# Sending half of the first batch's inner products by GpSimd's queue, and moving one chunk of the keys between two groups' scores

## The chip, the cores and the metric

The kernel runs on one core of one Trainium2 chip. The core has five engines that run beside one another: TensorE (PE in the profile) multiplies matrices, VectorE (DVE) and ScalarE (ACT) work element by element and on rows, GpSimd (POOL) does the same more slowly, and SyncE (SP) only issues transfers (DMAs). ACT and POOL issue transfers too. Each engine works through its own list of instructions in order: if one has to wait, all behind it on that engine wait with it. The metric is the time of one execution on the chip, in microseconds (us).

## The reference

For each of 8 batches there are 112 rows of queries (320 channels) and 375 rows of context (512 channels). The last 4 context rows are image prompts, the other 371 are text. There are 20 heads of 16 channels. In short form, with the mask called `m`:

```python
q, k, v   = x @ W_q, text @ W_k, text @ W_v          # by heads
probs     = softmax(q k^T / 4)                        # 112 x 371 for each head
text_out  = probs @ v
qsem      = l2norm(probs @ text)                      # 112 x 512 for each head
sem       = qsem @ l2norm(prompts)^T                  # 112 x 4 for each head
fused     = q (prompts @ W_k_ip)^T / 4 + 0.5 * sem
ip_out    = (softmax(fused) * m) @ (prompts @ W_v_ip)
out       = (text_out + ip_out) @ W_out + b_out + x
```

## The kernel before

The norm of `probs @ text` is not computed from the 512 channels. With the inner products of the context rows, `G = text text^T`, the squared norm is `p G p^T`, so for each head the kernel multiplies the probabilities by a matrix `u` whose columns are half of G (one triangle, doubled off the diagonal), then the inner products with the prompts, a column of ones and the head's 16 value channels. One product of 112 x 371 by 371 x 392 thus gives the norm, the prompts' part, the sum of the exponentials and the values. This is line 761 (`ps_qd<-u,xgT`).

TensorE works on 32 rows at a time there, four heads beside one another: a *group* is 4 heads, each batch has 5 groups, each group 12 blocks of 32 text rows. For that `u` has to lie in each of the four groups of 32 partitions (the *row groups*), and so has the transposed probability matrix `xgT`.

The names that matter for the first batch, in the order in which they come about:

- `first_gram` multiplies the turned context by itself (L491). `doubled` (L508 on ACT, L513 on POOL) writes the result to `ug`, 128 partitions of 792 columns.
- `gram_to_groups` (L543) copies `ug` to `u`: for each quarter `q` of its 128 partitions, four transfers of 99 KB, one for each row group. Four quarters make 16 transfers.
- `values` (L598) computes the values, ACT copies them to `vext` (L605), a transfer on ACT's queue writes them to `vd` in DRAM (L611), and `values_to_groups` (L632, four transfers on SP's queue) reads them back as `vr`. `placed` (L679, POOL) copies `vr` into its columns of `u`. The first of these copies needs all of `u` and all of `vr`.
- `project_queries` (L391) gives `qm` in three chunks of channels. The third, `ps_q_2`, reads columns of `wq_sb` that a copy on POOL fills (line 1090 before, 1091 after).
- `keys` (L559 and L576) gives `kT` in three chunks, `ps_k_0`, `ps_k_1` and `ps_k_2`. Groups 0 and 1 read the first chunk of `qm` and `kT`, groups 2 and 3 the second, group 4 the third.
- `scores` (L713) and `probabilities` (maximum L726 on DVE, exponential L730 on ACT, then a transfer `xg<-p`, L737 on SP) run per head. A score goes to one of the 8 banks of TensorE's output memory and can only start when that bank's former reader is done. `transposed` (L749, DVE) makes `xgT` of the group's four transfers, for group 0 in two halves of 6 blocks.
- `gram(1)` (L529) computes the inner products of batch 1, which `doubled` writes to the same `ug`, as soon as all 16 transfers have read it.
- After the prologue `alone(0)` runs group 0's 48 products with the scores of group 2 between them; then come a value chunk and a key chunk of batch 1, and `prompt_projections` (L304), which needs the weights `wip`. Those are two transfers of 640 KB (L125) on SP's queue, behind the transfers of group 1's probabilities.

The order of the prologue on each engine is the order in which the code is written; a generator such as `run(("k", 0), None)` emits one piece of its stage at a time.

Of the kernel before, what the change touches and what calls it, by code (L numbers as in the profile page):

```python
# [20 lines left out]
def kernel(  # L21
# [14 lines left out]
    nc = tc.nc  # L36
# [27 lines left out]
    QN = P // RG  # L64
# [105 lines left out]
    def load_turned(eng, bs):  # L170

        t0, n = blocks_of(bs)
        rows = x.rearrange("b s c -> (b s) c")[t0 : t0 + n * RG, :]
        for q in range(QN):
            eng.dma_start(
                x_in[q * RG : (q + 1) * RG, :n, :XW],
                rows[:, q * XW : (q + 1) * XW].rearrange("(j i) c -> i j c", i=RG),
            )
# [261 lines left out]
    def transposed_context(b):  # L440
        begin(b)
        s = st[b]
        ct, ctxT = s["ct"], s["ctxT"]
        if b > 0:

            for c in range(NT):
                some = slice(c * QN, (c + 1) * QN)
                nc.vector.transpose(  # L448
                    ctxT[:, :, c * P : (c + 1) * P].rearrange("p e (j i) -> p j e i", i=RG),
                    ct[:, some, :].rearrange("p j (k e) -> p j e k", e=NE),  # L450
                )
                if c == NT - 1:
                    prompts_behind(b)
                yield
            return
        for c in range(NT):
            rows = min(P, TT - c * P)
            ps = bank(f"ps_c_{b}_{c}")
            for e in range(NE):
                nc.tensor.transpose(  # L460
                    ps[:, e * P : e * P + rows],
                    chunk(ct[:, c, :], e)[:rows],
                    ident[:rows, :rows],
                )
            o = ctxT[:, :, c * P : c * P + rows]
            i = ps.rearrange("p (e t) -> p e t", t=P)[:, :, :rows]
            if c % 2:
                nc.vector.tensor_copy(o, i)
            else:
                nc.scalar.copy(o, i)  # L470
            yield
# [64 lines left out]
            doubled(ps, c, c, DEAL[c] if left_out(b, c) else ())  # L536
            yield

    def gram_to_groups(b, blocks):

        for q in blocks:
            for a in range(GROUP):
                nc.sync.dma_start(  # L543
                    st[b]["u"][a * RG : (a + 1) * RG, q * GW : (q + 1) * GW],
                    ug[q * RG : (q + 1) * RG, :],
                )
# [44 lines left out]
    def values(b):  # L591
        s = st[b]
        s["vext"] = work.tile([P, NT, C], F32, tag="vext", name=f"vext_{b}", bufs=1)
        ctxT, vext = s["ctxT"], s["vext"]
        for c in range(NT):
            ps = bank(f"ps_v_{b}_{c}")
            for e in range(NE):
                nc.tensor.matmul(  # L598
                    ps[:, :C],
                    ctxT[:, e, c * P : (c + 1) * P],  # L600
                    wv_sb[:, e, :],
                    start=(e == 0),
                    stop=(e == NE - 1),
                )
            nc.scalar.copy(vext[:, c, :], ps[:, :C])  # L605
            yield
# [68 lines left out]
    def placed(b, g, chunks=range(NT)):  # L675

        s = st[b]
        for c in chunks:
            nc.gpsimd.tensor_copy(  # L679
                region(b, c)[:, :, UV - c * P :], s["vr"][:, c * QN : (c + 1) * QN, g, :]  # L680
            )
# [19 lines left out]
    def scores(b, g, a, early=False, ps=None):  # L701
        s = st[b]
        _, qm, j = queries[b]
        i, r = g // 2, g % 2
        if early and (g + a // 2) % 2:

            ps = ps_qd.tile([P, 512], F32, tag="qd", name=f"ps_s_{b}_{g}_{a}")
        elif ps is None:
            ps = ps_sc.tile([P, 512], F32, tag="sc", name=f"ps_s_{b}_{g}_{a}")
        w = T if b > 0 else TT  # L710
        if i == FULL:
            r = a // 2
        nc.tensor.matmul(  # L713
            ps[:S, :w],
            qm[a * RG : (a + 1) * RG, i, r, j * S : (j + 1) * S],
            s["kT"][a * RG : (a + 1) * RG, i, :w],
            start=True,
            stop=True,
        )
        s["sc", g, a] = ps  # L720

    def probabilities(b, g, a):
        s = st[b]
        ps = s.pop(("sc", g, a))
        nmx = small.tile([S, 1], F32, tag="nmx", name=f"nmx_{b}_{g}_{a}", bufs=8)
        nc.vector.tensor_reduce(nmx, ps[:S, :TT], AX.X, ALU.max, negate=True)  # L726
        if ("p", g) not in s:
            s["p", g] = work.tile([S, GROUP, TT], F32, tag="p", name=f"p_{b}_{g}", bufs=4)
        p = s["p", g][:, a, :]
        nc.scalar.activation(p, ps[:S, :TT], AF.Exp, bias=nmx)  # L730
        if b > 0:
            nc.scalar.copy(s["ipl"][:, groups[g][a], :], ps[:S, TT:T])  # L732

        xg = x_ring[(b * NG + g) % NX]
        rows = xg[a * RG : a * RG + S // QN, :, :TT]
        eng = nc.scalar if (b, g, a) == (B - 1, NG - 1, GROUP - 1) else nc.sync
        eng.dma_start(rows, p)  # L737
# [315 lines left out]
    def drain(*gens):  # L1053
        for gen in gens:
            for _ in gen:
                pass
# [5 lines left out]
    def run(key, make, pieces=1):  # L1062

        if key not in gens:
            gens[key] = make()
        for _ in range(pieces):
            next(gens[key], None)
# [15 lines left out]
    turned_inputs(pairs[0])  # L1083
    drain(products)
    drain(transposed_context(1))
    gram_to_groups(0, range(QN - 1))
    run(("v", 0), lambda: values(0))
    run(("v", 0), None, 2)
    values_to_dram(0, nc.scalar)
# [5 lines left out]
    for a in range(GROUP):  # L1095
        scores(0, 0, a, early=True)
        probabilities(0, 0, a)
    gram_to_groups(0, (QN - 1,))
    run(("q", 0), None)
    for a in range(GROUP):  # L1100
        scores(0, 1, a, early=True)
        probabilities(0, 1, a)
# [1 line left out]
    load_embed(nc.sync, wvip_sb, w_v_ip)  # L1104
    transposed(0, 0)
    placed(0, 0)
    run(("k", 0), None, 2)
    load_turned(nc.gpsimd, pairs[1])
    more_constants()
    turn[:] = ["mm", "mm", "sc"]  # L1110
# [121 lines left out]
    def moved(b, g):  # L1232

        nb = b + 1
        if b % 2 == 0:
            if g in (1, 2):
                gram_to_groups(nb, (g - 1,))
            if g == 3:
                todo = [lambda: gram_to_groups(nb, (3,)), lambda: values_to_groups(nb)]
                for move in reversed(todo) if nb == B - 1 else todo:  # L1240
                    move()
        else:
            if g in (0, 1):
                gram_to_groups(nb, (g,))
            if g == 2:
                values_to_groups(nb, 0, 2)
# [114 lines left out]
    for n in range(0, len(steps) - NG, 2):  # L1361
# [4 lines left out]
        b, g = steps[n]  # L1366
# [16 lines left out]
    b = B - 1  # L1383
# [125 lines left out]
```

## Time and profile before

| what | us |
|---|---|
| three runs | 410.67, 411.17, 412.36 |
| median of the runs | 411.17 |
| span of the profiled execution | 409.5 |
| TensorE busy in that span | 402.0 |
| VectorE busy | 333.5 |
| ScalarE busy | 191.4 |
| GpSimd busy | 127.6 |

The span runs from the first to the last instruction of one profiled execution. The time of that one execution is not given apart from its span; the median of the runs lies 1.6 us above the span, and this is used for what lies around it. In the profile's rows of instructions in order of time the columns are start, duration, engine, line, operation, names, shapes and how many were merged; in brackets stands how long the engine was idle before and what ended that. `SPq` and `ACTq` are instructions that issue transfers on those queues; POOL's transfers are listed under POOL.

### The profile page before, as it was taken

How to read it: one execution, taken by the hardware profiler on the slowest of the kernel's cores; microseconds unless marked ns; L12 is line 12 of the kernel's file. 1: busy time of each engine (PE TensorE's matmuls, PEld its weight loads, DVE VectorE, ACT ScalarE, POOL GpSimd, SP SyncE). 2: the span in 40 equal slices, each digit the busy share in tenths (PEclk: the TensorE clock that was granted, in tenths of full speed). 3: DMA queues.
4: the chain of work that ended last, by engine and by line, in shares of the span. 5: the costliest groups of instructions: out<-in, count | busy, mean ns of one | idle time of the engine just before them, and what ended most of it. 6: DMA issues, size and time to landing. Idle time of an engine off the chain costs nothing.

```text
span 409.5 us, 14124 instructions
## 1 busy us (share of the span) xinstructions
PE 402.0 (98%) x5603; PEld 316.1 (77%) x5603; DVE 333.5 (81%) x705; ACT 191.4 (47%) x676; POOL 127.6 (31%) x294
## 2 busy tenths in 40 slices
PE   8998999999999999999999999999999999999996
PEld 8866687978777877878686877778777878787894
DVE  4354589877999898896899898887799988878985
ACT  3253234344533743434643574333734485346763
POOL 7203311322281153011154136002037135104681
PEclk9999999999999999999999999999999999999999
DMA  8876957799666866677646776666756444666310
GB/s 234 166 188 170 231 145 193 170 196 208 150 162 163 215 141 177 156 165 163 180 115 167 177 174 161 166 160 161 180 152 173 114 123 121 191 159 179 106 49 28
DMA packets 59332, 65.83 MB, mean 161 GB/s; under 512 B 20165, under 2 KB 52793, under 8 KB 59268
## 3 DMA queue, kind: packets, MB, share of 16 engines
q1 hardware_dynamic: 55326, 59.11, 58.4%
q0 software_dynamic: 1456, 3.14, 3.5%
q10 hardware_dynamic: 2486, 2.69, 2.1%
q8 instruction: 44, 0.72, 0.8%
q14 instruction: 20, 0.16, 0.1%
HBM read 20.22 MB, written 5.22 MB: 62 GB/s over the span
## 4 chain that ended last, share of the span: by engine, by line
PE 92%; DMA 3%; SPq 2%; POOL 1%; ACT 1%; issue 0%; DVE 0%; POOLq 0%
PE ps_qd L761 44%; PE ps_v L598 12%; PE ps_k L559 10%; PE ps_g L529 7%; PE ps_s L713 6%; PE ps_q L391 3%; PE ps_o L917 3%; DMA wip<-in_L_xattn_W_v_ip_dram 3%; PE ps_k L576 2%; PE ps_g L491 1%; SPq L737 1%; PE ps_w L477 1%; PE ps_c L460 1%; SPq L543 1%; PE ps_q L373 1%; PE ps_o L1013 0%
## 5 line engine op out<-in xcount | busy, mean ns | idle before, releaser
L761 PE MATMUL ps_qd<-u,xgT 32*112 32x136 f32 (+11 forms) x3840 | 216.4, 352 | 1.5 <-POOL u L679 1.1
L761 PEld LDWEIGHTS ps_qd<-u,xgT 32*112 32x112 f32 x3840 | 178.1, 172 | 36.4 <-issue 7.1
L749 DVE STREAM_TRANSPOSE xgT<-xg 128x768 f32<-128x768 f32 (+1 forms) x63 | 123.1, 1972 | 5.4 <-DMA xg<-p 5.1
L730 ACT ACTIVATE p<-ps_s,nmx 112x371 f32<-112x371 f32 x160 | 85.7, 585 | 56.9 <-DVE nmx L726 55.7
L726 DVE TENSOR_REDUCE nmx<-ps_s 112x1 f32<-112x371 f32 x160 | 77.2, 534 | 30.8 <-PE ps_s L713 28.9
L679 POOL COPY u<-vr 128x64 f32<-128x64 f32 x120 | 26.8, 237 | 190.9 <-PE ps_qd L761 113.8
L814 DVE CUSTOM_DVE_ANT_0 p<-ps_qd,p 112x371 f32<-112x371 f32 x152 | 73.6, 541 | 12.1 <-ACT pvs L788 7.4
L713 PE MATMUL ps_s<-kT,qm 32*112 32x375 f32 (+1 forms) x320 | 62.6, 485 | 0.0
L598 PE MATMUL ps_v<-wv_sb,ctxT 128*128 128x320 f32 x192 | 55.6, 437 | 0.0
L788 ACT COPY pvs<-ps_qd 112x21 f32<-112x21 f32 x152 | 21.8, 200 | 56.7 <-DVE ss L814 50.4
L598 PEld LDWEIGHTS ps_v<-wv_sb,ctxT 128*128 128x128 f32 x192 | 35.7, 190 | 14.3
L559 PE MATMUL ps_k<-ctxT,wk_sb 128*128 128x371 f32 x128 | 43.5, 483 | 0.0
L559 PEld LDWEIGHTS ps_k<-ctxT,wk_sb 128*128 128x128 f32 x128 | 23.1, 190 | 13.4 <-issue 1.3
L713 PEld LDWEIGHTS ps_s<-kT,qm 32*112 32x112 f32 x320 | 28.1, 171 | 5.7 <-ACT ug L508 0.4
L529 PE MATMUL ps_g<-ctxT 128*32 128x119 f32 (+11 forms) x672 | 32.4, 338 | 0.0
L529 PEld LDWEIGHTS ps_g<-ctxT 128*32 128x32 f32 x672 | 27.6, 109 | 5.9 <-issue 2.5
L448 DVE STREAM_TRANSPOSE ctxT<-ct 128x512 f32<-128x512 f32 x21 | 22.4, 1082 | 6.0 <-DMA u<-ug 6.0
L605 ACT COPY vext<-ps_v 128x320 f32<-128x320 f32 x24 | 10.2, 426 | 33.1 <-PE ps_v L598 24.5
L732 ACT COPY ipl<-ps_s 112x4 f32<-112x4 f32 x140 | 24.3, 173 | 0.0
L513 POOL TENSOR_TENSOR ug<-ug,half 128x128 f32<-128x128 f32 (+1 forms) x24 | 10.6, 448 | 29.7 <-ACT ug L512 27.6
L566 ACT COPY kT<-ps_k 128x371 f32<-128x371 f32 x16 | 7.5, 469 | 23.2 <-PE ps_k L559 22.8
L896 POOL TENSOR_TENSOR wv<-vip,w 112x1280 f32<-112x1280 f32 (+1 forms) x8 | 17.5, 2184 | 0.3 <-DVE w L890 0.3
(152 smaller groups left out, 326.0 us busy)
## 6 DMA issues: line engine op xcount, KB each, us to landing
xg<-p SPq DMA_DIRECT2D x159, 162.3 KB
u<-ug SPq DMA_DIRECT2D x128, 99.0 KB
ct<-in_ctx_dram SPq DMA_DIRECT2D x28, 176.0 KB
vip<-vipd SPq DMA_DIRECT2D x7, 560.0 KB
vr<-vd SPq DMA_DIRECT2D x20, 120.0 KB
out_dram<-ob SPq DMA_DIRECT2D x7, 140.0 KB
vd<-vext ACTq DMA_DIRECT2D x12, 80.0 KB
vr<-vd SPq DMA_DIRECT2D x12, 80.0 KB
```

The lines of the kernel that those rows point to most:

```text
L448: nc.vector.transpose(ctxT[:, :, c * P : (c + 1) * P].rearrange("p e (j i) -> p j e i", i=RG), ct[:, some, :].rearrange("p j (k e) -> p j ...
L529: nc.tensor.matmul(ps[p * RG : (p + 1) * RG, s0 : T - t0], ctxT[:, e, t0 + q * RG : t0 + (q + 1) * RG], ctxT[:, e, t0 + s0 : T], start=(e ...
L559: nc.tensor.matmul(ps[:, :TT], wk_sb[:, e, i * P : (i + 1) * P], s["ctxT"][:, e, :TT], start=(e == 0), stop=(e == NE - 1),)
L598: nc.tensor.matmul(ps[:, :C], ctxT[:, e, c * P : (c + 1) * P], wv_sb[:, e, :], start=(e == 0), stop=(e == NE - 1),)
L679: nc.gpsimd.tensor_copy(region(b, c)[:, :, UV - c * P :], s["vr"][:, c * QN : (c + 1) * QN, g, :])
L713: nc.tensor.matmul(ps[:S, :w], qm[a * RG : (a + 1) * RG, i, r, j * S : (j + 1) * S], s["kT"][a * RG : (a + 1) * RG, i, :w], start=True, st ...
L726: nc.vector.tensor_reduce(nmx, ps[:S, :TT], AX.X, ALU.max, negate=True)
L730: nc.scalar.activation(p, ps[:S, :TT], AF.Exp, bias=nmx)
L732: nc.scalar.copy(s["ipl"][:, groups[g][a], :], ps[:S, TT:T])
L749: nc.vector.transpose(xT[:, j : j + n].rearrange("p j (k q) -> p q j k", q=QN), xg[:, :, j * RG : (j + n) * RG].rearrange("p q (j k) -> p ...
L761: nc.tensor.matmul(banks[a][:S, j * RG : UW], xT[a * RG : (a + 1) * RG, j, :S], region(b, c)[a * RG : (a + 1) * RG, p, q * RG :], start=(j ...
L814: nc.vector.tensor_tensor_reduce(out=p, in0=ps[:S, :TT], in1=p, scale=1.0, scalar=0.0, op0=ALU.mult, op1=ALU.add, accum_out=s["ss"][:, h : ...
```

## The change

Two things move in the first batch's prologue, and nothing is added or taken out of the computation. `gram_to_groups` gets a parameter for the engine that issues. The 16 transfers of `ug` were issued by SP, twelve directly after `ug` was made and four behind the probabilities of group 0. Now SP issues eight directly, and POOL the other eight (quarters 2 and 3), at its place in the program. The keys' second chunk, which stood with the third behind the scores of group 1, now stands ahead of them.

```diff
-    def gram_to_groups(b, blocks):
+    def gram_to_groups(b, blocks, eng=nc.sync):
 
         for q in blocks:
             for a in range(GROUP):
-                nc.sync.dma_start(
+                eng.dma_start(
                     st[b]["u"][a * RG : (a + 1) * RG, q * GW : (q + 1) * GW],
                     ug[q * RG : (q + 1) * RG, :],
                 )
...
     drain(transposed_context(1))
-    gram_to_groups(0, range(QN - 1))
+    gram_to_groups(0, (0, 1))
+    gram_to_groups(0, (2, 3), nc.gpsimd)
     run(("v", 0), lambda: values(0))
...
     for a in range(GROUP):
         scores(0, 0, a, early=True)
         probabilities(0, 0, a)
-    gram_to_groups(0, (QN - 1,))
     run(("q", 0), None)
+    run(("k", 0), None)
     for a in range(GROUP):
         scores(0, 1, a, early=True)
         probabilities(0, 1, a)
...
     placed(0, 0)
-    run(("k", 0), None, 2)
+    run(("k", 0), None)
     load_turned(nc.gpsimd, pairs[1])
```

In the lists below a number behind a name is only its place in the program, and `x4` is four equal instructions. First TensorE before, from the last score of group 0 (`ps_s_0_3`) over the third query chunk and group 1's scores (`ps_s_1_*`) to the keys' chunks:

```order
L713 MATMUL ps_s_0_3_350<-kT_168,qm_305 112x371
L391 MATMUL ps_q_2_360<-xT_222,wq_sb 128x112 x3
L713 MATMUL ps_s_1_0_367<-kT_168,qm_305 112x371
L713 MATMUL ps_s_1_1_374<-kT_168,qm_305 112x371
L713 MATMUL ps_s_1_2_380<-kT_168,qm_305 112x371
L713 MATMUL ps_s_1_3_386<-kT_168,qm_305 112x371
L559 MATMUL ps_k_1_400<-ctxT_166,wk_sb 128x371 x4
L576 MATMUL ps_k_2_406<-ctxT_166,wk_sb 64x186
```

The same place on TensorE now:

```order
L713 MATMUL ps_s_0_3_354<-kT_168,qm_309 112x371
L391 MATMUL ps_q_2_360<-xT_222,wq_sb 128x112 x3
L559 MATMUL ps_k_1_367<-ctxT_166,wk_sb 128x371 x4
L713 MATMUL ps_s_1_0_373<-kT_168,qm_309 112x371
L713 MATMUL ps_s_1_1_380<-kT_168,qm_309 112x371
L713 MATMUL ps_s_1_2_386<-kT_168,qm_309 112x371
L713 MATMUL ps_s_1_3_392<-kT_168,qm_309 112x371
L576 MATMUL ps_k_2_406<-ctxT_166,wk_sb 64x186
```

The four matmuls of `ps_k_1` have moved ahead of the four scores; `ps_q_2` still stands ahead of both.

GpSimd before, from its part of the first inner products (L513) over the prompts' copy behind batch 1's context (L436) to the next loads:

```order
L513 TENSOR_TENSOR ug<-ug,half 128x115
L436 COPY ctxT_259<-ipnT 128x4x4
L1090 COPY wq_sb<-wq_sb 128x3x64
L679 COPY u_170<-vr_171 128x4x16 x3
L175 DMA x_in<-in_x_dram 32x7x80 x4
```

The same place on GpSimd now:

```order
L513 TENSOR_TENSOR ug<-ug,half 128x115
L436 COPY ctxT_259<-ipnT 128x4x4
L543 DMA u_170<-ug 32x792 x8
L1091 COPY wq_sb<-wq_sb 128x3x64
L679 COPY u_170<-vr_171 128x4x16 x3
L175 DMA x_in<-in_x_dram 32x7x80 x4
```

The eight issues stand behind the copy of L436, which waits for DVE, and ahead of the copy into `wq_sb` on which `ps_q_2` waits.

SP's queue before, from the loads of batch 1's context (L143) to the prompts' weights:

```order
L143 DMA ct_112<-in_ctx_dram 19x128 x4
L543 DMA u_170<-ug 32x792 x12
L632 DMA vr_171<-vd_169 32x12x80 x4
L737 DMA xg_140<-p_0_335 28x4x371 x4
L543 DMA u_170<-ug 32x792 x4
L737 DMA xg_142<-p_1_371 28x4x371 x4
L125 DMA wip<-in_L_xattn_W_k_ip_dram 128x1280
L125 DMA wip<-in_L_xattn_W_v_ip_dram 128x1280
```

The same place on SP's queue now:

```order
L143 DMA ct_112<-in_ctx_dram 19x128 x4
L543 DMA u_170<-ug 32x792 x8
L632 DMA vr_171<-vd_169 32x12x80 x4
L737 DMA xg_140<-p_0_339 28x4x371 x4
L737 DMA xg_142<-p_1_377 28x4x371 x4
L125 DMA wip<-in_L_xattn_W_k_ip_dram 128x1280
L125 DMA wip<-in_L_xattn_W_v_ip_dram 128x1280
```

Eight transfers of `ug` have left SP's queue, four from ahead of `vr` and four from between the probabilities of the two groups.

## The prediction

> **What bounds the kernel now.** I read the page first, for the shares of the engines.
>
> ```profile
> span 409.5 us, 14124 instructions
> PE 402.0 (98%) x5603; PEld 316.1 (77%) x5603; DVE 333.5 (81%) x705; ACT 191.4 (47%) x676; POOL 127.6 (31%) x294
> ```
>
> TensorE counts as busy nearly throughout, so there are two ways to gain time: remove the few waits that are left, or remove time that counts as busy but is stretched. The waits of TensorE, in the view of who waited for whom, are five; these two lie where the change is:
>
> ```profile
> PE ps_qd L761 <- POOL u L679: 1.1, 1, 1.1
> PE ps_kv L304 <- DMA wip<-in_L_xattn_W_v_ip_dram: 0.4, 1, 0.4
> ```
>
> Stretched time shows only in the rows in order of time. TensorE from group 0's scores to the first product of group 0, with one weight load (PEld) and the prompts' projection at the end:
>
> ```profile
> 24.05 0.89 PE L713 MATMUL ps_s<-kT,qm 32*112 32x371 f32 x8
> 24.87 0.92 PE L391 MATMUL ps_q<-xT,wq_sb 128*128 128x112 f32 x6
> 25.72 1.77 PE L713 MATMUL ps_s<-kT,qm 32*112 32x371 f32 x8
> 27.42 2.76 PE L559 MATMUL ps_k<-ctxT,wk_sb 128*128 128x371 f32 x8
> 30.11 1.47 PE L576 MATMUL ps_k<-ctxT,wk_sb 128*64 128x186 f32 x16
> 31.52 4.65 PE L529 MATMUL ps_g<-ctxT 128*32 128x375 f32 x96
> 37.25 0.93 PE L761 MATMUL ps_qd<-u,xgT 32*112 32x392 f32 x8 [1.08 <-POOL u L679]
> ...
> 38.62 0.17 PEld L713 LDWEIGHTS ps_s<-kT,qm 32*112 32x112 f32 x1 [0.44 <-ACT ug L508]
> ...
> 49.04 1.28 PE L304 MATMUL ps_kv<-wip,ipT 128*32 128x160 f32 x28 [0.42 <-DMA wip<-in_L_xattn_W_v_ip_dram]
> ```
>
> Taken from start to start, the same eight score instructions need 0.82 us in group 0 (24.05 to 24.87) and 1.70 us in group 1 (25.72 to 27.42): group 1's wait there for banks that group 0's exponentials still read. So 0.88 us is stretch. Then TensorE idles 1.08 us ahead of group 0's products, because GpSimd places the values late, and that because the last four blocks of `u` land late; ScalarE waits for the same transfers before it may overwrite `ug`:
>
> ```profile
> 36.95 0.59 POOL L679 COPY u<-vr 128x64 f32<-128x64 f32 x3 [15.72 <-DMA u<-ug]
> ...
> 37.06 0.40 ACT L508 ACTIVATE ug<-ps_g 128x279 f32<-128x279 f32 x1 [4.15 <-DMA u<-ug]
> ```
>
> Being late there, ScalarE also holds a bank that a score of group 2 needs (the 0.44 us at 38.62). What that stage loses in all is seen beside a later one of the same make, two groups with their eight scores in 50.25 to 61.10:
>
> ```profile
> core 0: us, PE busy (x), PEclk, DMA share, GB/s
> 37.25:43.31 6.06, 6.06 (x104) 1.00 0.84 238
> 50.25:61.10 10.85, 10.81 (x210) 1.00 0.65 155
> ```
>
> Half of 10.85 is 5.43, against 6.06 for one group with four scores: 0.63 us lost, 0.44 of it directly seen. The clock is full in both.
>
> **The change, part by part.** The rows of the two queues:
>
> ```profile
> 14.95 10.12 SPq L543 DMA_DIRECT2D u<-ug  x12
> 21.37 0.67 SPq L543 DMA_DIRECT2D u<-ug  x1
> 23.92 0.51 SPq L543 DMA_DIRECT2D u<-ug  x1
> 25.11 2.16 SPq L632 DMA_DIRECT2D vr<-vd  x4
> 27.36 3.70 SPq L737 DMA_DIRECT2D xg<-p  x4
> 31.12 2.48 SPq L543 DMA_DIRECT2D u<-ug  x4
> 33.70 3.92 SPq L737 DMA_DIRECT2D xg<-p  x4
> 38.26 0.43 SPq L125 DMA_DIRECT2D wip<-in_L_xattn_W_v_ip_dram  x1
> ...
> 9.16 0.73 POOL L198 DMA_DIRECT2D wq_sb<-in_L_xattn_W_q_dram  x1
> 10.41 0.51 POOL L198 DMA_DIRECT2D wq_sb<-in_L_xattn_W_q_dram  x1
> 20.54 0.20 POOL L436 COPY ctxT<-ipnT 128x16 f32<-128x16 f32 x1 [6.01 <-DVE ctxT L448]
> 20.88 0.35 POOL L1090 COPY wq_sb<-wq_sb 128x192 f32<-128x192 f32 x1
> 37.55 2.40 POOL L175 DMA_DIRECT2D x_in<-in_x_dram  x4
> ```
>
> *Eight issues on GpSimd.* They cannot begin before 20.74, the end of the copy at 20.54. One issue there costs from 0.51 us (row at 10.41) to 0.73 us (row at 9.16); four larger ones take 2.40, or 0.60 each. The 0.73 row overlaps a VectorE copy from SBUF to SBUF:
>
> ```profile
> 9.37 0.76 DVE L259 COPY wv_sb<-wv_in 128x512 f32<-128x512 f32 x2 [0.46 <-DMA wv_in<-in_L_xattn_W_v_dram]
> ```
>
> I take 0.52, since these transfers have 32 rows, between the small and the large ones, and VectorE has no such copy in 20.7 to 25. Eight are 4.2, the copy into `wq_sb` (0.35) ends at 25.3 where it ended at 21.23, and `ps_q_2`, at 24.87 before, starts 0.4 us late; at 0.73 it would be 2.1 late, and that is the bound. Behind `ps_q_2` stands all of TensorE. The Trainium skill (SBUF — State Buffer, "SBUF: two separate sides") says that a VectorE fp32 copy within SBUF locks GpSimd out, so that it cannot write descriptors; the 0.73 row agrees. If the four `qm` operations (L400) in that window locked it too, at about 0.29 us each, the sum below would be some 1.1 us worse; the page VectorE: DVE Perf Modes ("Why `tensor_tensor` can't do 2×_2P or 4×") excludes it for operands in PSUM, which these have.
>
> *The keys' chunk ahead of group 1's scores.* It reads nothing new, and the 2.69 us of `ps_k_1` (27.42 to 30.11) give group 0's exponentials time to free the banks: the 1.70 becomes 0.82. TensorE then runs `ps_q_2` 25.3 to 26.1, `ps_k_1` to 28.8, scores to 29.6, `ps_k_2` (1.41) to 31.0, batch 1's inner products (4.65) to 35.7.
>
> *SP's queue.* Ten of the twelve issues are over at 22.04, so eight end near 20.7. The next, `vr`, needs `vd`; the eleventh issue at 23.92 seems to have waited for the same transfer. So `vr` is issued at 23.9 to 26.1, some 1.2 us earlier than before, then group 0's probabilities until 29.8 instead of 31.06. When they have landed is seen at VectorE:
>
> ```profile
> 25.53 1.95 ACT L730 ACTIVATE p<-ps_s,nmx 112x371 f32<-112x371 f32 x4 [0.52 <-DVE nmx L726]
> 33.53 1.65 DVE L749 STREAM_TRANSPOSE xgT<-xg 128x768 f32<-128x768 f32 x1 [4.40 <-DMA xg<-p]
> ```
>
> The exponentials end at 27.48, in time. Landing came 2.47 us after the last issue (33.53 less 31.06): 32.3 now, if nothing is in the way. But the four blocks that were issued behind these probabilities now travel ahead of or beside them. Their price is between nothing and 2.48, the row at 31.12. I take 1.2, as GpSimd's transfers start before `vr` is even issued. The first half of `xgT` is then ready at 33.5 + 1.65 = 35.2, at worst 36.4, against 35.7 for TensorE. `u` and `vr` are no longer last: with the last block issued at 25, they would have to take over 10 us to land to matter.
>
> *First product.* 37.25 becomes 35.7: 0.88 + 1.08 less 0.4 for `ps_q_2`, **1.6 us**. Then ScalarE is free to empty batch 1's inner products as they come, and the stage loses less: **0.5**, between the 0.44 seen and the 0.63 worked out.
>
> *The prompts' weights.* In the chain of work that ended last they stand as
>
> ```profile
> 38.26 10.74 DMA wip<-in_L_xattn_W_v_ip_dram
> ```
>
> Group 1's exponentials ended 3.43 us after the first score in group 0 (24.05 to 27.48), so now near 32.2; SP, free from 29.8, takes 3.92 for the four, and the second weights are issued at about 34.3 and land at 45.0. TensorE would ask for them at 48.6 less 2.1, or 46.5. The **0.4** us go, with 1.5 to spare.
>
> Behind that, the chain is TensorE's own work, so the 2.5 us stay. 409.5 − 1.6 − 0.5 − 0.4 = 407.0 for the span, and with the 1.6 us by which the median of the runs (411.17) lies above it, 408.7.
>
> **The rivals.** First, *slower*: GpSimd's issues are slow, and TensorE stands at `ps_q_2`. The price is eight times what one issue takes above 0.52; all is lost at 0.83 each, and half a per cent (2.06 us, about what a measurement of this kernel can tell from no change) at 1.09. For it: SP's ten took 0.71 each for the same shape, as the transfers held them up. Against it: GpSimd's own rows lie at 0.51 to 0.73 beside busy transfers. At 0.71 each the loss would be 1.5 and the time 410.2; at 1.2 each, 8 × 0.68 = 5.4 us, 414.1.
>
> Second, *the transfers take the wait's place*: group 0's probabilities land late. With all four blocks ahead, the first half of `xgT` comes at 36.4, and if `vd`, which now shares the engines with GpSimd's blocks, lands a microsecond later too, at 37.4, where the wait for `u` ended before. Only the 0.5 and 0.4 are left: 410.3. For it: transfers on GpSimd's queue were slow beside full ones, as the loads at 37.55 show:
>
> ```profile
> DMA to landing us min/median/max: 4.4/6.9/9.9
> ```
>
> Against it: those ran beside 1.3 MB of weights. The Trainium skill (DMA: Bandwidth & Descriptors, "Issuing engines are not separate DMA queues") speaks for this rival: a second issuing engine saves only issue time, all share the same 16 engines. By that rule alone the gain would be the one that this rival gives.
>
> Third, *given back*: the earlier loads at 37.55 would now meet group 1's probabilities and the prompts' weights, so that the wait at 49.04 stays or grows by up to what was won ahead of it: 409.1 to 411.2.
>
> **How the numbers follow.** My forecast, 408.0 to 409.6 with 408.7 as likeliest, gets 0.57; of that 0.45 lies below 409.1, half a per cent under the median, and 0.12 above it. The second rival gets 0.18 and the third 0.10, both within half a per cent; the first 0.15, of which 0.10 is slower by more than that and 0.05 within. This makes 0.45 faster, 0.45 within, 0.10 slower. The range from 407.9 to 411.4 leaves out the slow first rival and a gain above 3.3 us.
>
> **What would show it.** Right: `ps_q_2` near 25.3; group 1's scores in about 0.8 us; no wait for `u` ahead of the first L761, which starts near 35.7; no wait of L304 for `wip`. The first rival would show as a long row of L543 on POOL and an idle TensorE ahead of L391; the second as a first L761 that waits for VectorE's L749; the third as a longer wait at L304. The forecast falls most easily by the landing of the probabilities, for which the trace has no like case.

## The result: 1.6 us faster, and the profile after

The median of nine runs is 409.43 us (408.17 to 410.35), beside 411.05 us (410.29 to 412.36) for nine runs of the kernel before. The quotient of the two medians is 0.9961. The recorded ratio, another estimate from the same runs, is 0.9953 with a 95% interval from 0.9942 to 0.9964; the ratios further down are of this kind. The gain is thus 0.39 to 0.47%, just inside the half per cent that the prediction took for no change. The forecast was 408.7 us, 0.6% faster. One execution of a kernel further down took 584.97 us at a granted clock of 0.658; it is left out of that kernel's figures, and its trace is not read. The page of the changed kernel:

```profile
span 407.4 us, 14134 instructions
PE 401.0 (98%) x5603; PEld 318.6 (78%) x5603; DVE 332.3 (82%) x705; ACT 191.2 (47%) x676; POOL 131.6 (32%) x302
```

The span is 2.1 us shorter, more than the median gained. The time around the span grew: it is 1.99 to 2.07 us in the nine executions of the change, and 1.66 to 1.76 in 45 executions of the kernel before. So about 0.3 us is given back outside the first and the last instruction; no run shows by what. TensorE's busy time fell by 1.0 us with as many instructions: that is stretch. In the view of who waited for whom, the wait for `wip` is gone, and the one at the first product of group 0 is shorter:

```profile
PE ps_a L908 <- POOL attn L903: 0.6, 1, 0.6
PE ps_qd L761 <- POOL ug L513: 0.5, 1, 0.5
```

TensorE in order of time, from group 0's scores on, with one row of its weight loads and the prompts' projection:

```profile
14.20 6.63 PE L598 MATMUL ps_v<-wv_sb,ctxT 128*128 128x320 f32 x24
...
24.70 0.89 PE L713 MATMUL ps_s<-kT,qm 32*112 32x371 f32 x8
25.52 0.92 PE L391 MATMUL ps_q<-xT,wq_sb 128*128 128x112 f32 x6
26.28 2.67 PE L559 MATMUL ps_k<-ctxT,wk_sb 128*128 128x371 f32 x8
28.88 0.89 PE L713 MATMUL ps_s<-kT,qm 32*112 32x371 f32 x8
29.70 1.47 PE L576 MATMUL ps_k<-ctxT,wk_sb 128*64 128x186 f32 x16
31.11 4.93 PE L529 MATMUL ps_g<-ctxT 128*32 128x375 f32 x96
36.49 1.22 PE L761 MATMUL ps_qd<-u,xgT 32*112 32x392 f32 x10 [0.45 <-POOL ug L513]
...
33.51 2.33 PEld L529 LDWEIGHTS ps_g<-ctxT 128*32 128x32 f32 x64 [0.38 <-ACT kT L586]
...
46.69 1.29 PE L304 MATMUL ps_kv<-wip,ipT 128*32 128x160 f32 x32
```

Group 1's scores now take 0.82 us from start to start (28.88 to 29.70). But the inner products of batch 1 (L529) take 4.93 us where they took 4.65: their weight loads stood 0.38 us at 33.51 for a bank that ScalarE empties at L586. That is the copy of the keys' third chunk, which on ScalarE now stands behind group 1's exponentials. Then TensorE idles 0.45 us ahead of the first L761. The queues and the engines that feed that product:

```profile
19.14 0.20 POOL L436 COPY ctxT<-ipnT 128x16 f32<-128x16 f32 x1 [3.96 <-DVE ctxT L448]
19.69 3.97 POOL L543 DMA_DIRECT2D u<-ug  x8 [0.35 <-issue]
23.65 0.36 POOL L1091 COPY wq_sb<-wq_sb 128x192 f32<-128x192 f32 x1
30.37 0.59 POOL L679 COPY u<-vr 128x64 f32<-128x64 f32 x3 [6.36 <-DMA vr<-vd]
...
15.21 5.10 SPq L543 DMA_DIRECT2D u<-ug  x8
26.14 1.87 SPq L632 DMA_DIRECT2D vr<-vd  x4
28.11 7.29 SPq L737 DMA_DIRECT2D xg<-p  x8
36.05 0.52 SPq L125 DMA_DIRECT2D wip<-in_L_xattn_W_v_ip_dram  x1
...
21.33 0.41 ACTq L611 DMA_DIRECT2D vd<-vext  x1
32.19 1.26 ACT L586 COPY kT<-ps_k 64x186 f32<-64x186 f32 x4
34.75 1.64 DVE L749 STREAM_TRANSPOSE xgT<-xg 128x768 f32<-128x768 f32 x1 [3.06 <-DMA xg<-p]
```

The values are placed in `u` by 31.0 (30.37 and 0.59), long before they are needed. What comes last is the first half of `xgT`: VectorE waits for the probabilities until 34.75 and is done at 36.39, and TensorE starts 0.10 us later. The row names a GpSimd instruction (L513) as what ended the wait. That is most likely a coincidence in time: the same product started 0.10 and 0.11 us after the same half of `xgT` in two traces of kernels below, and there L244 is named. The probabilities are late because SP issues them behind `vr`, and `vr` waits for `vd`, which the chain of work that ended last shows:

```profile
21.33 4.75 DMA vd<-vext
```

The stage that begins with the first product, up to group 1's first product. The columns are the stretch, TensorE's busy time, its granted clock, the busy share of the DMA engines and what they moved:

```profile
core 0: us, PE busy (x), PEclk, DMA share, GB/s
36.49:41.84 5.35, 5.35 (x104) 1.00 0.99 291
41.84:47.91 6.07, 6.07 (x52) 1.00 0.95 209
```

The same two stretches of before are the 6.06 that the prediction shows, and this one, in the same columns:

```profile
43.31:50.25 6.94, 6.52 (x51) 1.00 1.00 199
```

So from first product to first product 13.00 us became 11.42.

### The profile page after: what moved, and what is told of

It is laid out like the page before. It is cut to its first block, busy times and chain, and to the rows that moved or that the text cites. A ratio compares the mean times of both kernels' runs of the same rounds, so it can differ in the third digit from the quotient of the medians.

```text
span 407.4 us, 14134 instructions
## 1 busy us (share of the span) xinstructions
PE 401.0 (98%) x5603; PEld 318.6 (78%) x5603; DVE 332.3 (82%) x705; ACT 191.2 (47%) x676; POOL 131.6 (32%) x302
## 4 chain that ended last, share of the span: by engine, by line
PE 92%; DMA 3%; POOL 3%; issue 0%; SPq 0%; ACT 0%; DVE 0%; POOLq 0%
PE ps_qd L761 46%; PE ps_v L598 13%; PE ps_k L559 9%; PE ps_s L713 6%; PE ps_g L529 6%; PE ps_o L917 3%; PE ps_q L391 2%; PE ps_k L576 2%; PE ps_g L491 1%; DMA vd<-vext 1%; DMA xg<-p 1%; DMA ct<-in_ctx_dram 1%; DMA vr<-vd 1%; PE ps_c L460 1%; POOL x_in L175 1%; PE ps_q L373 1%
## 5 line engine op out<-in xcount | busy, mean ns | idle before, releaser
L761 PE MATMUL ps_qd<-u,xgT 32*112 32x40 f32 (+11 forms) x3840 | 216.4, 352 | 0.7 <-POOL ug L513 0.5
L761 PEld LDWEIGHTS ps_qd<-u,xgT 32*112 32x112 f32 x3840 | 180.3, 172 | 33.6 <-issue 6.9
L679 POOL COPY u<-vr 128x64 f32<-128x64 f32 x120 | 26.9, 237 | 188.2 <-PE ps_qd L761 118.2
L713 PE MATMUL ps_s<-kT,qm 32*112 32x375 f32 (+1 forms) x320 | 60.9, 486 | 0.0
L598 PE MATMUL ps_v<-wv_sb,ctxT 128*128 128x320 f32 x192 | 55.6, 437 | 0.0
L598 PEld LDWEIGHTS ps_v<-wv_sb,ctxT 128*128 128x128 f32 x192 | 35.7, 190 | 14.2
L529 PE MATMUL ps_g<-ctxT 128*32 128x119 f32 (+11 forms) x672 | 32.7, 338 | 0.0
L529 PEld LDWEIGHTS ps_g<-ctxT 128*32 128x32 f32 x672 | 27.7, 110 | 6.1 <-issue 1.8
L513 POOL TENSOR_TENSOR ug<-ug,half 128x128 f32<-128x128 f32 (+1 forms) x24 | 10.6, 446 | 28.9 <-ACT ug L512 27.0
```

The lines of the kernel that those rows point to most:

```text
L529: nc.tensor.matmul(ps[p * RG : (p + 1) * RG, s0 : T - t0], ctxT[:, e, t0 + q * RG : t0 + (q + 1) * RG], ctxT[:, e, t0 + s0 : T], start=(e ...
L598: nc.tensor.matmul(ps[:, :C], ctxT[:, e, c * P : (c + 1) * P], wv_sb[:, e, :], start=(e == 0), stop=(e == NE - 1),)
L679: nc.gpsimd.tensor_copy(region(b, c)[:, :, UV - c * P :], s["vr"][:, c * QN : (c + 1) * QN, g, :])
L713: nc.tensor.matmul(ps[:S, :w], qm[a * RG : (a + 1) * RG, i, r, j * S : (j + 1) * S], s["kT"][a * RG : (a + 1) * RG, i, :w], start=True, st ...
L761: nc.tensor.matmul(banks[a][:S, j * RG : UW], xT[a * RG : (a + 1) * RG, j, :S], region(b, c)[a * RG : (a + 1) * RG, p, q * RG :], start=(j ...
```

## The experiments

Two things were open. What ends the wait of 0.45 us that is left, and which edit would remove it: fewer transfers on GpSimd, or the same ones earlier? And what is each of the two edits worth alone? Edits are given against the changed kernel. "Distance" is the time on TensorE from the start of the values (L598) to the first L761 of group 0. It is used because L598 itself starts between 13.45 and 14.26 in traces whose work up to there is the same, so that a start by the clock carries that scatter. For before it is 37.25 − 13.55 = 23.70 us, for the change 36.49 − 14.20 = 22.29.

| kernel | ratio to before, 95% | distance | idle ahead of the first L761 |
|---|---|---|---|
| before | 1 | 23.70 | 1.08 |
| the change | 0.9953 (0.9942 to 0.9964) | 22.29 | 0.45 |
| the change, once more | 0.9953 (0.9936 to 0.9969) | 22.62 | 0.78 |
| queue part only | 0.9937 (0.9916 to 0.9959) | 22.55 | 0 |
| keys' part only | 0.9994 (0.9972 to 1.0015) | 24.20 | 2.35 |
| twelve on SP, four on GpSimd | 0.9973 (0.9945 to 1.0001) | 22.71 | 0.87 |
| all sixteen on GpSimd | 1.0101 (1.0075 to 1.0127) | 28.25 | 0, but 4.31 ahead of `ps_q_2` |
| copy into `wq_sb` first | 0.9927 (0.9903 to 0.9952) | 22.01 | 0.18 |
| eight ahead of batch 1's context | 0.9913 (0.9893 to 0.9933) | 21.77 | 0 |
| the same, once more | 0.9933 (0.9907 to 0.9959) | not read | not read |
| the same, keys as before | 0.9938 (0.9922 to 0.9954) | 22.55 | 0 |
| the same, both key chunks ahead | 0.9917 (0.9900 to 0.9934) | 21.48 | 0 |

### The queue part alone

```diff
     run(("q", 0), None)
-    run(("k", 0), None)
     for a in range(GROUP):
         scores(0, 1, a, early=True)
...
-    run(("k", 0), None)
+    run(("k", 0), None, 2)
```

> The transfers are divided as in the change, the keys' second chunk stays behind group 1's scores. My theory: TensorE's path (group 1's scores stretched to 1.7 us again) ends 0.9 us later than in the change, but 0.45 us of that was idle there ahead of the first L761, so about 0.5 us is lost: ratio to the kernel before about 0.9965. First L761 no longer waits. Rival, that the two parts pay separately and the keys' part is worth its whole 0.9 us: 0.9975. Rival, that the queue alone makes the whole gain: 0.995.

Measured: 409.51 us, ratio 0.9937. TensorE in order of time:

```profile
32.13 4.65 PE L529 MATMUL ps_g<-ctxT 128*32 128x375 f32 x96
36.72 1.22 PE L761 MATMUL ps_qd<-u,xgT 32*112 32x392 f32 x10
```

There is no wait ahead of the product, L529 takes its old 4.65, and the product starts as far from the values as in the change, within the scatter of one trace (22.55 beside 22.29 and 22.62). The half microsecond that was expected to be lost is not: within the intervals the queue part alone carries the whole gain. What the keys' part saves in the change goes into the wait for the probabilities and the 0.28 at L529.

### The keys' part alone

```diff
-    gram_to_groups(0, (0, 1))
-    gram_to_groups(0, (2, 3), nc.gpsimd)
+    gram_to_groups(0, range(QN - 1))
...
+    gram_to_groups(0, (QN - 1,))
     run(("q", 0), None)
     run(("k", 0), None)
```

> All transfers on SP's queue as before, only the keys' second chunk stands ahead of group 1's scores. My theory: TensorE is done 0.9 us earlier and then waits that much longer for the last four blocks of u, so the ratio is 1.000 (0.999 to 1.001) and the wait of the first L761 grows from 1.1 to about 2 us. Rival, that the parts pay separately: 0.998.

Measured: 411.19 us, ratio 0.9994. The wait at the first product, in the view of who waited for whom:

```profile
PE ps_qd L761 <- POOL u L679: 2.4, 1, 2.4
```

and its row in order of time:

```profile
37.65 0.93 PE L761 MATMUL ps_qd<-u,xgT 32*112 32x392 f32 x8 [2.35 <-POOL u L679]
```

TensorE gets there earlier and waits longer for the same placing of the values (L679) behind the last blocks of `u`: 2.35 instead of 1.08. The traced execution took 412.38 us, 1.2 above the median, so its wait may be longer than that of most. Without the queue part this edit is worth nothing that the runs can tell.

### Twelve on SP, four on GpSimd

```diff
-    gram_to_groups(0, (0, 1))
-    gram_to_groups(0, (2, 3), nc.gpsimd)
+    gram_to_groups(0, (0, 1, 2))
+    gram_to_groups(0, (3,), nc.gpsimd)
```

> Twelve transfers by SP, four by GpSimd, keys as in the change. In the change vd takes 4.75 us to land and vr is issued at 26.1, later than before. If that is because GpSimd's eight transfers share the engines with vd, then with four on GpSimd vd lands sooner, vr goes out near 25.1, group 0's probabilities land near 34 instead of 34.75, and the 0.45 us of idle TensorE ahead of the first L761 go: ratio 0.994. Rival, the engines carry the same bytes in either case: vr is held up by SP's own twelve, ratio 0.9955 as the change or a little worse.

Measured: 410.04 us, ratio 0.9973. The transfer of the values from the chain that ended last, SP's queue and the first product:

```profile
21.38 3.84 DMA vd<-vext
...
15.26 11.14 SPq L543 DMA_DIRECT2D u<-ug  x12
26.44 2.16 SPq L632 DMA_DIRECT2D vr<-vd  x4
...
36.97 1.22 PE L761 MATMUL ps_qd<-u,xgT 32*112 32x392 f32 x10 [0.87 <-POOL attn L244]
```

The idea was that fewer transfers on GpSimd let `vd` and with it `vr` through earlier. Of its two steps the first came true in this trace: `vd` took 3.84 us beside 4.75 in the change. The second fell. SP's own twelve issues now end at 26.40, and `vr` goes out behind them at 26.44, no earlier than in the change (26.14); the idle time is 0.87, no shorter. With twelve, SP's own issues are late by themselves.

### Eight on GpSimd, ahead of batch 1's context

```diff
     drain(products)
+    gram_to_groups(0, (2, 3), nc.gpsimd)
     drain(transposed_context(1))
     gram_to_groups(0, (0, 1))
-    gram_to_groups(0, (2, 3), nc.gpsimd)
```

> As the change, but GpSimd issues its eight before the copy that waits for batch 1's turned context: from about 15.2 instead of 19.7 us. My theory: all 16 blocks travel before vd starts, vd lands in under 3 us, vr and group 0's probabilities come 1 to 2 us earlier, the first L761 does not wait: 0.45 us better than the change, ratio 0.994. Rival, the 16 engines were already full from 16 to 22 us, so the blocks finish no sooner and batch 1's context or vd is pushed back instead: same as the change or slower, 0.9955 to 0.998.

Measured: 408.33 us, ratio 0.9913. GpSimd, SP's queue, VectorE and TensorE:

```profile
15.03 3.98 POOL L543 DMA_DIRECT2D u<-ug  x8 [0.29 <-POOL ug L513]
...
24.59 1.87 SPq L632 DMA_DIRECT2D vr<-vd  x4
...
33.32 3.08 DVE L749 STREAM_TRANSPOSE xgT<-xg 128x768 f32<-128x768 f32 x2 [2.08 <-DMA xg<-p]
...
35.53 1.22 PE L761 MATMUL ps_qd<-u,xgT 32*112 32x392 f32 x10
```

GpSimd no longer stands behind the copy of L436, which waits for VectorE, and its eight are issued at 15.03 instead of 19.69. `vr` leaves 10.83 us after the start of the values (24.59 − 13.76), 11.94 in the change; the probabilities follow, and the wait is gone. The same kernel once more, beside before on another chip:

> The kernel with GpSimd's eight ahead of the copy that waits for batch 1's context, and the second key chunk ahead of group 1's scores, once more: 0.9913 as in its first sitting if that was not the sitting's; 0.9935 if the sitting made it look better, as the kernel before was slower there (411.59).

It gave 408.79 us (the median of the five executions that count) and 0.9933; the two intervals overlap, and the second overlaps that of the change.

### The same with the keys as before, and with both key chunks ahead

Both keep the eight ahead of batch 1's context. The first puts the keys' second chunk back behind group 1's scores:

```diff
     run(("q", 0), None)
-    run(("k", 0), None)
...
-    run(("k", 0), None)
+    run(("k", 0), None, 2)
```

> GpSimd issues its eight ahead of batch 1's context copy, and the keys' second chunk stands behind group 1's scores as in the kernel before. My theory: the keys' part paid little in the change because the transposes of group 0 were the later of the two; with the transfers out of the way TensorE's own path sets the start of the first L761, so taking the keys' part back costs its 0.88 us less the 0.28 us that batch 1's inner products lose in the other order, 0.6 us: 0.993 where the same kernel with the keys ahead gave 0.9913. Rival, the keys' part is worth nothing in any case: 0.9913.

The second puts the third chunk ahead of those scores as well:

```diff
     run(("q", 0), None)
-    run(("k", 0), None)
+    run(("k", 0), None, 2)
...
-    run(("k", 0), None)
```

> GpSimd's eight ahead of the context copy, and both remaining key chunks ahead of group 1's scores. My theory: ScalarE then empties the third chunk's bank before group 1's exponentials, and the 0.28 us stall in batch 1's inner products goes: 0.9906 where the second chunk alone ahead gave 0.9913. Rival: group 1's probabilities come 1.4 us later, so the prompts' weights behind them land late and TensorE waits for them again: 0.992 or worse.

On one chip, beside the change once more:

> The changed kernel itself, once more beside the others: ratio 0.9953 as measured. It gives the distance to the other three from one sitting, and a second trace that shows what of the first one (the loads 0.65 us late, 0.45 us idle ahead of the first L761) belongs to the kernel and what to one execution.

Measured: 409.04 us (0.9938) with the keys as before, 407.97 us (0.9917) with both chunks ahead, 409.58 us (0.9953) for the change. TensorE with both chunks ahead:

```profile
30.40 4.65 PE L529 MATMUL ps_g<-ctxT 128*32 128x375 f32 x96
34.98 1.22 PE L761 MATMUL ps_qd<-u,xgT 32*112 32x392 f32 x10
...
45.18 1.29 PE L304 MATMUL ps_kv<-wip,ipT 128*32 128x160 f32 x32
```

With the transfers out of the way, the order of the keys is worth 409.04 − 407.97 = 1.07 us, and the distance shows as much (22.55 − 21.48 = 1.07; that the two agree to the last digit is chance). Five of the six runs with both chunks ahead lie under all six with the keys as before, though the two intervals overlap. L529 is back at 4.65, since ScalarE now copies the third key chunk ahead of group 1's exponentials. L304 does not wait, although the weights are issued later there. The kernel with both chunks ahead is 1.6 us under the change on the same chip, with intervals that just part (0.9934 and 0.9936). Against the kernel with one key chunk ahead (0.9913 and 0.9933) it is not told apart.

### All sixteen on GpSimd

```diff
-    gram_to_groups(0, (0, 1))
-    gram_to_groups(0, (2, 3), nc.gpsimd)
+    gram_to_groups(0, range(QN), nc.gpsimd)
```

> All 16 transfers on GpSimd's queue. This prices the wait of the third query chunk behind GpSimd's issues. My theory: 16 issues of 0.5 us from 19.7 end at 27.7, the third query chunk starts near 28.1 instead of 25.5, and TensorE loses about 2.1 us against the change: ratio 1.000. [...] Rival, TensorE has slack there: 0.9955.

Measured: 414.84 us, ratio 1.0101. TensorE's longest wait:

```profile
PE ps_q L391 <- POOL wq_sb L1090: 4.3, 1, 4.3
```

GpSimd's issues and the row of the waiting matmuls, in order of time:

```profile
20.13 4.96 POOL L543 DMA_DIRECT2D u<-ug  x10 [0.35 <-issue]
25.72 2.59 POOL L543 DMA_DIRECT2D u<-ug  x5 [0.63 <-DMA u<-ug]
...
29.36 1.62 PE L391 MATMUL ps_q<-xT,wq_sb 128*128 128x112 f32 x6 [4.31 <-POOL wq_sb L1090]
```

This is the wait of the prediction's first rival, made to happen by the number of issues. Sixteen issues push the copy into `wq_sb` behind 28.9, `ps_q_2` waits 4.31 us for it, and the kernel is 3.4 us slower than before on this chip and 5.3 slower than the change. That is more than the 2.1 us that were expected. The issues themselves still cost 0.50 us each; the wait of 0.63 ahead of the eleventh is for an earlier transfer. The rest is stretch behind the wait: `ps_q_2` and the key chunk took 5.74 us (1.62 and 4.12) where they take 3.59 in the change (0.92 and 2.67), at a clock that the last section shows.

### The copy into `wq_sb` first

```diff
     gram_to_groups(0, (0, 1))
+    nc.gpsimd.tensor_copy(wq_sb[:, :, C:], wq_sb[:, :, FULL * P : C])
     gram_to_groups(0, (2, 3), nc.gpsimd)
...
-    nc.gpsimd.tensor_copy(wq_sb[:, :, C:], wq_sb[:, :, FULL * P : C])
```

> As the change, but GpSimd makes its copy into wq_sb ahead of its eight issues, so the third query chunk never waits for them. Both traces of the change show no such wait; if that is so in most executions, nothing changes: 0.9953. If the wait comes back in executions where batch 1's context lands later (the copy ahead of the issues ended at 22.4 in one other trace, which would put the third query chunk at 26.8), the median gains up to a microsecond: 0.993.

Measured: 408.30 us, ratio 0.9927. The first product:

```profile
35.49 1.22 PE L761 MATMUL ps_qd<-u,xgT 32*112 32x392 f32 x10 [0.18 <-POOL attn L244]
```

The interval (0.9903 to 0.9952) overlaps that of the change. In this trace `vr` leaves 10.64 us after the start of the values (24.12 − 13.48), sooner than with the eight ahead, although the eight stand behind the copy of L436 here. In the change's own traces `ps_q_2` does not wait, so nothing in them says that this edit must gain; whether it does is not settled.

## Why the prediction was right, and where it was wrong

The span was forecast at 407.0 and came out at 407.4, and at 407.7 in the second trace of the change. The median fell by 1.62 us and not by 2.5. Of the 0.7 us by which it lies above the forecast, about half is span; the other half is the time around the span, 2.0 us where the forecast carried over the 1.67 between before's median and span. Against the start of the values the forecast's terms compare so:

| term | forecast | the change | once more |
|---|---|---|---|
| up to the first product | −1.6 | −1.41 | −1.08 |
| from there to group 1's first product | −0.9 | −1.58 | −1.57 |
| values started later in this trace | | +0.65 | +0.41 |
| given back behind | 0 | +0.20 | +0.37 |
| sum, at the kernel's end | −2.5 | −2.14 | −1.87 |

That the total came as near as it did is partly luck: the first term fell short by 0.2 to 0.5 us and 0.2 to 0.4 were given back, while the second paid 0.7 more than forecast.

*Eight issues on GpSimd: the price was right, the 0.4 us were not lost.* An issue cost 0.50 us (3.97 for eight) where 0.52 was taken. Two of VectorE's `qm` operations (L400, 0.58 us from 21.53) ran beside them and did not hold them up: with the eight ahead, where none ran beside them, eight issues took 3.98. That an operand in TensorE's output memory (PSUM) keeps VectorE out of the mode that takes both of its read ports is stated by the Trainium skill in VectorE: DVE Perf Modes, "Why PSUM operands drop a tier", and not in the section that the prediction names. The issues started at 19.69 and not at 20.74, as batch 1's context came sooner, and `ps_q_2` stands 11.32 us behind the start of the values as before (25.52 − 14.20, 24.87 − 13.55). The copy at L436 stood 6.99 us behind the values' start in before and 8.78 with the keys' part alone, and 4.94 to 6.04 in the six traces in which GpSimd issues blocks behind it. Whether the change itself brings that context sooner was not tried.

*The keys' part: the stretch went, its gain did not arrive.* The stretch went from 1.70 to 0.82 as said, and the sum counted all of the 0.88. But the change (409.43 and 409.58 us) is no faster than its queue part alone (409.51), because the first product then waits for the probabilities. Not foreseen either was that the third key chunk, left behind group 1's scores, holds a bank of L529 by ScalarE's queue: 0.28 us, which the kernel with both chunks ahead gets back.

*The step that failed: "So `vr` is issued at 23.9".* It was 26.14, and 25.94 once more, later than the 25.11 of before also against the start of the values (11.94 and 11.98 us behind it, 11.56 in before). The reading of before under it holds. In the view of who waited for whom, an issue of `u` on SP's queue waited 1.9 us for `vd`; that is the eleventh, from 22.04 to 23.92. Just behind it the DMA engines moved nothing (a busy share of 0.01 and 0 GB/s, the last two columns):

```profile
SPq L543 <- DMA vd<-vext: 1.9, 1, 1.9
...
24.00:24.50 0.50, 0.50 (x10) 1.00 0.01 0
```

So by this view `vd` had landed by 23.92, 3.24 us after its issue at 20.68. What failed is that the change was given the same 3.2 us. With GpSimd's blocks in the same window `vd` took 4.75 us, and 4.79 once more. The last of group 0's probabilities was issued by 31.81 (forecast 29.8; 1.4 us late against the start of the values), and they landed at 34.75 where 33.5 was forecast, 0.6 us late in that count. The rest was covered by an allowance that was too large: landing took 2.94 us and not the 2.47 + 1.2 of the forecast. So 0.45 us (0.78 once more) of the 1.08 stayed, waiting for something else: the second rival, in part. The Trainium skill (DMA: Bandwidth & Descriptors, "Issuing engines are not separate DMA queues") says that a second issuing engine saves only issue time, and this part of the result agrees. From the issue of `vd` to that of `vr`, the kernels with the eight ahead show 3.56 to 3.71 us; those with the eight behind show 4.81, 4.85, 4.32 in the queue part alone and 3.52 with the copy first. With four behind, `vd` took the 3.84 shown above. That the blocks slow `vd` is thus supported by all traces but one, and not shown.

*Sums.* 0.88 + 1.08 − 0.4 = 1.6 was forecast up to the first product; it was 0.88, plus 0.18 at the seams of the keys' chunk, less 0.28 at L529, plus 1.08 − 0.45 = 0.63: 1.41.

*The stage behind it and the prompts' weights: right, both too small.* Group 0's stage fell by 6.06 − 5.35 = 0.71, where 0.5 was taken and 0.63 worked out. The weights were issued at 36.05, not 34.3, and still in time. Their wait, taken at its idle 0.42, was worth more: from the first L304 to group 1's first product 2.09 us (48.16 to 50.25) became 1.22 (46.69 to 47.91), 0.87 less. TensorE's rows count a part of such a wait as busy.

*Third rival.* The earlier loads did not bring the wait at L304 back. Only 0.20 to 0.37 us were lost behind it. In the second trace of the change 0.30 of the 0.37 is one wait, of batch 1's first product for the placing of batch 1's values, which the first trace and that of before don't have:

```profile
85.53 1.22 PE L761 MATMUL ps_qd<-u,xgT 32*112 32x392 f32 x10 [0.30 <-POOL u L679]
```

Why that placing comes late there was not tried.

## What to carry to other kernels

Moving issues from a crowded queue to an idle one pays by what stood behind them on the crowded one. It is worth trying them ahead of any instruction that waits on the new queue: placed so, the 0.45 to 0.78 us that were left of the wait here were gone. That the placing is the cause rests on two traces with the keys' chunk ahead, and the copy put first came near to it without (0.18). A reordering that shortens one stage is worth nothing until the transfer behind the next wait comes sooner too, so try such pairs together and apart. And how long a transfer took before (`vd`, 3.24 us) is not how long it takes when the change puts other transfers into its window (4.75): give such a term a price of its own, and not only a rival.

## What the hardware showed unexpectedly

TensorE's granted clock (PEclk, 1.00 is full speed) fell at or after an idle stretch. With all sixteen on GpSimd TensorE idled from 25.05 to 29.36; the clock was down to 0.50 by 27.0, and behind the wait it went on so:

```profile
core 0: us, PE busy (x), PEclk, DMA share, GB/s
29.30:30.80 1.50, 1.44 (x7) 0.50 1.18 228
30.80:34.90 4.10, 4.10 (x13) 0.65 1.01 204
34.90:37.00 2.10, 2.10 (x24) 1.00 0.60 131
```

The six matmuls of `ps_q_2` took 1.62 us there instead of 0.92. With the keys' part alone, behind 2.35 us of waiting, in the same columns:

```profile
37.60:40.40 2.80, 2.75 (x21) 0.75 0.83 241
40.40:42.00 1.60, 1.60 (x16) 0.50 1.02 329
42.00:45.40 3.40, 3.40 (x79) 0.94 0.99 231
```

Read in finer stretches, the clock there is 1.00 until 38.8 and 0.50 from 39.2 to 42.2, so it fell some 1.4 us behind the end of the wait (37.65). Group 0's stage took 7.73 us (37.65 to 45.38) instead of 6.06, so in that execution the longer wait cost more than its length. In the traces of before and of the change, behind waits of 1.08 and 0.45 us, the clock stayed at 1.00. The Trainium skill (TensorE: Matmul & The Clock Gate, "HAM oscillation — how this bites in real kernels") states the rule as "no PE-idle gaps >~3.4µs"; the 4.31 us agree, though the clock fell within the first 2 us of them.

Whether 2.35 us is enough by itself is not shown. The mean granted clock of each execution is on record: with all sixteen on GpSimd it is 0.992 in all six, but with the keys' part alone it is 0.994 to 0.996 in three of twelve (the traced one is among them) and at least 0.999 in the other nine. Such a drop also turned up where the traced wait is shorter, in three of twelve executions with twelve and four (0.992 to 0.996; they took 412.61 to 414.90 us, the other nine 408.90 to 410.57) and in three of 45 of the kernel before (0.996), and in none of the 50 in which GpSimd issues eight (0.998 and more). By an estimate from the stretches above, 3.4 us at half clock in 411 us make a mean of 0.996.
